# Taking the node tables' products apart in PSUM, with kv writes that wait for no window load

## The chip, the cores and the metric

The kernel runs on one core of one Trainium2 chip. The metric is the device time of one execution in microseconds (us). Three executions of the kernel before gave 5036.83, 5021.88 and 5028.19 us, so the median is 5028.19 us. One more execution was profiled: 5024.54 us, with a span of 5022.8 us from its first to its last instruction and a mean granted TensorE clock of 0.904.

## The reference

One layer of a graph network over 12,500 nodes with 128 features, 412,500 edges sorted by destination (each edge, its reverse and one loop per node), and 64 features per edge:

```
h, q, k, v = x @ Wn + bn, x @ Wq + bq, x @ Wk + bk, x @ Wv + bv
eh   = edge_features @ We + be
hmid = leaky_relu(concat(q[src], k[dst], eh) @ A1 + b1, 0.2)
s    = leaky_relu(hmid @ A2 + b2, 0.2).mean(-1)
w    = softmax(s over all edges)
out  = segment_sum(w * v[dst], by src)
y    = layernorm(x + gamma * norm(h + out) + beta)
```

Wq, Wk and We are multiplied with their parts of A1 once, on the chip, so that q, k and the edge part add up directly to the hidden layer. What the change touches is the node tables: for every node a row of k and v (256 numbers), a row of q (128) and a row of h (128). Rows of q, k and v are kept as three bf16 pieces whose sum is the float32 number: the first piece is the number rounded to bf16, the second the rest rounded, the third what is then left.

## The kernel before

**Stages.** Nodes lie in 98 blocks of 128; seven blocks (NB = 7) make one of 14 node groups (ng). Edges are cut into 403 groups of 1,024, in destination order, and the edge groups into six parts of 51 to 73 groups. While part p is spread out, part p-1 is reduced.

- Spreading out (`make`, called once per part): for each edge group, `load` fetches edge features, destinations and a window of 128 piece rows of the k, v table; `onehots`, `masked` and `places` on VectorE work out where each edge goes; `rows` on TensorE picks k, v with one-hot matrices and adds the edge part; `evacuate` copies the result to SBUF on ScalarE (tile `rec`, six buffers, four edge tiles each); and GpSimd issues one indirect DMA (L904, "scatter" below) for each of the eight edge tiles, into the table `rtab` of the part, ordered by source block.
- Reducing (`sums_of`, from part 1 on): for blocks of source nodes the rows of `rtab` are loaded again (`rt`, L1038), and TensorE, VectorE and ScalarE do the hidden layer, the scores, the softmax weights and the weighted sums. At the end `closing` does the two norms.

The load of the first `rt` of a part reads rows that all scatters of that part have written, so it waits for the last of them.

**The tables.** The k, v rows of node group 0 are made before everything else, by code that keeps the product in PSUM and takes it apart there (L686 to L695). The other 27 jobs, k, v of node groups 1 to 13 and then q, h of node groups 0 to 13, are the generator `tables()`, whose steps are strewn between the steps of part 0: a part's generator `make` yields six times per edge group, so part 0 has 306 steps, and the tables' 379 steps are spread evenly over the first 275 of them. The small tables on edges (`edges`, chunks of 52 edge groups) and the zero fills of `rtab` (L522) are strewn in the same way. All engines run their instructions in the order in which this interleaving emits them, and every DMA that is not a scatter is issued by the SP queue, in order.

A job of `tables()` before: load the seven blocks of x, transposed (L1519, two buffers). Per block one float32 matmul into PSUM (L1534, two buffers `ph`) and one VectorE add of the bias into the SBUF tile `ns` (L1539). Then `parts3` on the whole group: ScalarE rounds to bf16 (L1502), VectorE subtracts into `less` (L1507), ScalarE rounds, VectorE subtracts, ScalarE rounds. All pieces lie in the tile `sp`, which has one buffer. Then the writes: `kvtab` (L1547) for a k, v job, `htab` (L1557) and `qtab` (L1558) for a q, h job.

The window load of an edge group (L796) reads `kvtab` at a row that is known only at run time, so it counts as reading the whole table. A load therefore waits for the last `kvtab` write in front of it, and a `kvtab` write waits for all window loads in front of it. `made_rows` records how many node groups' rows were written when a load was issued; `covered` checks at the end that no window reached beyond.

## Time and profile before

| what | value |
|---|---|
| median of three runs | 5028.19 us |
| profiled execution | 5024.54 us, span 5022.8 us |
| busy: TensorE, VectorE, ScalarE, GpSimd | 4158.4, 3991.7, 3267.8, 3348.4 us |
| scatters (L904) | 3224, the first at 31.3 us, the last at 4331.6 us |
| scatters of part 0 | 408 of them (51 edge groups) |

Times in the rows are microseconds from the start of the span unless they are marked ns. A group's row gives the line, engine and operation, the tiles written and read, how often it ran, then busy time, mean duration in ns, and idle time of the engine in front of it with what ended that idle time. A row of stretches gives for each engine the busy time in the stretch and, in brackets, the instructions; then the granted TensorE clock, the share of time for which the 16 DMA engines were busy, and the GB/s moved. A row of waits gives who waited for what: microseconds in total, how often, the longest. "issue" marks time in which nothing that the profile shows was waited for.

### The profile page before, as it was taken

What the parts mean: (1) busy time and instruction counts of PE and PEld (TensorE: products, weight loads), DVE (VectorE), ACT (ScalarE), POOL (GpSimd) and SP (SyncE); (2) the same over time, 40 slices, a digit from 0 to 9 for tenths busy, and PEclk for the clock granted to TensorE, in tenths of its full rate; (3) what the DMA queues carried; (4) which work ended last, traced back from release to release, by engine and by line L of the source; (5) the groups of instructions that cost most, each with busy time, mean ns of one, the idle gap of its engine ahead of it and who ended that gap; (6) DMA issues with size and microseconds to landing.
All of it is one profiled execution on the core that took longest, in us unless ns stands there. A gap on an engine that the chain in (4) does not pass through costs nothing.

```text
span 5022.8 us, 97600 instructions
## 1 busy us (share of the span) xinstructions
PE 4158.4 (83%) x32218; PEld 3108.6 (62%) x32676; DVE 3991.7 (79%) x10036; ACT 3267.8 (65%) x8495; POOL 3348.4 (67%) x3268
## 2 busy tenths in 40 slices
PE   4565578898888888799998898999899999899980
PEld 3333356666566666577776676676667777667760
DVE  7877576788777777688888888888888888677778
ACT  3433255666566666577777777777677777677876
POOL 5777777777777777777777777777777777410002
PEclk7777588899999999899999999999999999999995
DMA  7999799998899988899989888989899999788763
GB/s 262 314 318 344 255 328 333 343 312 300 274 324 324 329 301 289 275 318 318 313 308 311 302 315 311 309 307 313 301 306 314 315 324 318 265 287 283 262 224 141
DMA packets 614992, 1505.49 MB, mean 300 GB/s; under 512 B 103587, under 2 KB 328246, under 8 KB 612681
## 3 DMA queue, kind: packets, MB, share of 16 engines
q1 hardware_dynamic: 459433, 1069.47, 65.0%
q0 software_dynamic: 154752, 429.39, 22.7%
q8 instruction: 259, 4.24, 0.3%
q14 instruction: 260, 2.13, 0.1%
q10 hardware_dynamic: 288, 0.26, 0.0%
HBM read 929.49 MB, written 608.37 MB: 306 GB/s over the span
## 4 chain that ended last, share of the span: by engine, by line
DMA 37%; PE 24%; DVE 16%; POOL 9%; issue 6%; ACT 6%; SPq 1%; DVEq 0%; ACTq 0%; POOLq 0%
DMA rtab<-rec,idx 14%; DMA rt<-rtab 13%; POOL rtab L904 9%; PE psm L1268 6%; DMA row<-slT 4%; PE ph L1116 4%; PE pkv L881 3%; PE ph L1107 3%; DMA rowB<-row 3%; DVE hm L1131 2%; PE psc L1144 2%; PE pkv L875 2%; ACT rec L892 2%; PE psm L1177 2%; ACT ohw L1239 2%
## 5 line engine op out<-in xcount | busy, mean ns | idle before, releaser
L904 POOL DMA_INDIRECT rtab<-rec,idx x3224 | 3286.2, 1019 | 1042.0 <-issue 781.0
L892 ACT ACTIVATE rec<-pkv 128x1024 f32<-128x1024 f32 x806 | 819.9, 1017 | 863.5 <-PE pkv L881 475.4
L1239 ACT ACTIVATE ohw<-ohs,w 128x128 f32<-128x128 bf16 x3822 | 1258.7, 400 | 58.4 <-DVE ohs L1225 47.9
L1268 PE MATMUL psm<-rt,ohw 128*128 128x128 f32 x7644 | 1158.6, 294 | 10.7 <-ACT ohw L1239 10.6
L1268 PEld LDWEIGHTS psm<-rt,ohw 128*128 128x128 f32 x7644 | 997.5, 200 | 59.5 <-ACT ohw L1239 17.7
L1127 ACT ACTIVATE hm<-ph 128x512 f32<-128x512 f32 (+1 forms) x1078 | 581.7, 540 | 461.6 <-PE ph L1116 429.0
L1116 PE MATMUL ph<-ohT,qs 128*128 128x512 bf16 (+3 forms) x3658 | 718.1, 312 | 25.5 <-issue 2.6
L1131 DVE TENSOR_TENSOR hm<-ph,hm 128x512 f32<-128x512 f32 (+1 forms) x1078 | 668.5, 620 | 83.3 <-ACT hm L1127 81.9
L875 PE MATMUL pkv<-kvs,ohd 128*128 128x256 bf16 x3224 | 531.4, 292 | 204.0 <-ACT rec L892 189.7
L1107 PE MATMUL ph<-ident,rt 128*128 128x128 f32 x3822 | 629.3, 283 | 45.8 <-DVE hm L1131 43.4
L881 PE MATMUL pkv<-WeS,eat 64*128 64x128 f32 x6448 | 633.6, 320 | 0.0
L1096 DVE TENSOR_SCALAR ohT<-rowB,iotaP 128x512 bf16<-128x512 uint8 (+1 forms) x1078 | 518.4, 481 | 102.1 <-DMA rowB<-row 97.2
L881 PEld LDWEIGHTS pkv<-WeS,eat 64*128 64x128 f32 x6448 | 467.9, 205 | 191.8 <-issue 184.9
L875 PEld LDWEIGHTS <-ohd 128*128 128x128 bf16 x3224 | 316.2, 103 | 317.5 <-issue 224.5
L1107 PEld LDWEIGHTS ph<-ident,rt 128*128 128x128 f32 x3822 | 471.9, 152 | 64.1 <-DVE hm L1131 51.0
L1116 PEld LDWEIGHTS <-qs 128*128 128x128 bf16 x4116 | 396.8, 100 | 129.4 <-issue 4.8
L1225 DVE TENSOR_TENSOR ohs<-iotaE,sl 128x512 bf16<-128x512 bf16 (+1 forms) x1078 | 427.1, 396 | 48.4 <-ACT ohw L1239 46.8
L844 DVE TENSOR_TENSOR ats<-pc,oh 128x792 f32<-128x792 f32 x403 | 392.1, 973 | 82.1 <-PE pc L826 76.9
L1144 PE MATMUL psc<-hm,A2s 128*32 128x512 f32 (+3 forms) x2352 | 337.7, 538 | 80.1 <-DVE slT L1075 75.9
L1177 PE MATMUL psm<-headsum,z 128*128 128x4 f32 (+1 forms) x2156 | 287.9, 255 | 128.0 <-DVE part L1284 87.0
L855 DVE TENSOR_REDUCE pos<-ats 128x8 f32<-128x792 f32 x403 | 390.2, 968 | 4.2
L1177 PEld LDWEIGHTS psm<-headsum,z 128*128 128x128 f32 (+1 forms) x2156 | 280.9, 202 | 149.4 <-DVE part L1284 102.6
(161 smaller groups left out, 4080.2 us busy)
## 6 DMA issues: line engine op xcount, KB each, us to landing
rt<-rtab SPq DMA_DIRECT2D x196, 1820.0 KB
eat<-in_ea SPq DMA_DIRECT2D x201, 512.0 KB
rt<-rtab SPq DMA_DIRECT2D x49, 1560.0 KB
rt<-rtab SPq DMA_DIRECT2D x49, 1300.0 KB
qs<-qtab SPq DMA_DIRECT2D x294, 192.0 KB
rtab<-rec,idx POOLq DMA_INDIRECT x3224
dstb<-dtab SPq DMA_DIRECT2D x201, 256.0 KB
rtab<-empty SPq DMA_DIRECT2D x98, 520.0 KB
```

Of the source, the lines that this page charges most:

```text
L875: nc.tensor.matmul(pk[:, h, i, :], ohd[:, t * P : (t + 1) * P], kvs, start=(i == 0), stop=False,)
L881: nc.tensor.matmul(pk[:, h, i, :D], eat[h * DE : (h + 1) * DE, (j + i) * P : (j + i + 1) * P], WeS[h * DE : (h + 1) * DE, :], start=False, ...
L892: nc.scalar.activation(rec[:, :, :, : 2 * D], pk, AF.Copy)
L904: one_tile = nc.gpsimd.indirect_dma_start(out=rtab[p % TABS][:, :], out_offset=bass.IndirectOffsetOnAxis(ap=idxs[g][:, t : t + 1], axis=0) ...
L1096: nc.vector.tensor_scalar(st["oh"][k][:, : n * P], st["rowB"][:, t0 * P : (t0 + n) * P], iotaP, None, op0=ALU.is_equal,)
L1107: nc.tensor.matmul(ph[:, j * P : (j + 1) * P], st["rt"][:, t0 + j, :D], ident, is_transpose=True, start=(j == 0), stop=False,)
L1116: nc.tensor.matmul(ph[:, cols], st["qs"][:, j0 // t, s, :], oh[:, cols], start=False, stop=(s == 2 and j1 == t0 + n),)
L1127: nc.scalar.activation(hm, state[i]["ph", k][:, : n * P], AF.Copy, scale=SLOPE)
L1131: nc.vector.tensor_tensor(hm, ph[:, : n * P], hm, op=ALU.max)
L1177: nc.tensor.matmul(st["psS"][:, t0 + j : t0 + j + (nv - 1) * sw + 1 : sw], z[: 32 * nv, j * P : (j + 1) * P], headsum[: 32 * nv, :nv], sta ...
L1239: nc.scalar.activation(ohw[:, j, :], ohs[:, :, j], AF.Copy, scale=st["w"][:, t0 + j : t0 + j + 1])
L1268: nc.tensor.matmul(st["psS"][:, (1 + u) * P : (2 + u) * P], ohw[:, j, :], st["rt"][:, t0 + j, D : 2 * D], start=(k == 0), stop=(k == t - 1),)
```

## The change

- **Products.** A job's seven blocks are now four products, of two, two, two and one blocks. A product's matmuls write one PSUM bank. Banks come in turn from the pools `ph` (twice), `psc` and `psm`, which have nothing else to do in part 0, so four products can be in flight.
- **Bias.** VectorE adds it in place in PSUM (`biased`): for k, v jobs to the v half alone (k's bias is zero in this formulation, as in the code for node group 0), for q, h jobs to both halves.
- **Pieces.** Per product: ScalarE rounds PSUM to `sp` (`rounded`), VectorE subtracts in place in PSUM (`left`, s = 0), ScalarE rounds again, VectorE subtracts from PSUM straight into the third piece of `sp` (`left`, s = 1). The tiles `ns` and `less` and the third rounding are gone. For q, h jobs ScalarE also copies h from PSUM to SBUF (`own`).
- **Order.** An explicit table of 225 slots, two per product, strewn like the 379 steps before over the first 275 steps of part 0: product at slot t, bias at t + 1, rounding at t + 2, first subtraction at t + 4, second rounding at t + 5, second subtraction at t + 6, and the job's writes two slots after its last subtraction. x is loaded eight slots, one job, ahead.
- **Buffers.** `sp` has two (`sp0`, `sp1`), h has two.
- **Waits on the k, v table.** A window load is told not to depend on writes of node groups from `ready[g]` on, and a `kvtab` write not to depend on any window load. `made_rows` now lags by one node group, so a load depends on writes up to the one before the latest. A no-op stands in front of each `kvtab` write on the SP queue.
- **Edge tables.** In `edges` the write of `dtab` (L609) is issued one step later, behind all four VectorE instructions instead of between them.

```diff
@@ -606,13 +606,13 @@
         )
         db = tmp.tile([size, EG], U8, name="db")
         nc.vector.tensor_scalar(db[:m, :], dI[:m, :], first[:m, :], None, op0=ALU.subtract)
-        nc.sync.dma_start(out=dtab[g0:g1, :], in_=db[:m, :])
         dl = tmp.tile([size, EG], BF, name="dl")
         nc.vector.tensor_scalar(dl[:m, :], dI[:m, :], first[:m, :], None, op0=ALU.subtract)
         row = tmp.tile([size, 1], I32, name="row")
         nc.vector.tensor_scalar(row[:m, :], first[:m, :], 3.0, None, op0=ALU.mult)
+        yield
+        nc.sync.dma_start(out=dtab[g0:g1, :], in_=db[:m, :])
         nc.sync.dma_start(out=stab[g0:g1, :], in_=row[:m, :])
-        yield
         nc.vector.tensor_reduce(mm[:m, 0, c : c + 1], dl[:m, :], AX.X, ALU.max)
         yield
         nc.vector.tensor_reduce(mm[:m, 1, c : c + 1], dl[:m, :], AX.X, ALU.min)
@@ -672,7 +672,7 @@
             psmp.tile([P, 4 * P], FP, name="psm"),
             pkvp.tile([P, 2, 2, 2 * D], FP, name="pkv").rearrange("p h i w -> p (h i w)"),
         ]
-        sp = np_.tile([P, NB, 3, 2, D], BF, name="sp")
+        sp = np_.tile([P, NB, 3, 2, D], BF, name="sp1")
         for b in range(0, NB, 2):
             m = min(2, NB - b)
             at = nodes[b // 2][:, : 2 * D * m]
@@ -793,10 +793,13 @@
                 skip_runtime_bounds_check_because="starts are held within the table on the chip",
             )
             kvs = kvp.tile([P, 2 * D], BF)
-            nc.sync.dma_start(
+            read = nc.sync.dma_start(
                 out=kvs,
                 in_=kvtab.rearrange("n (s w) -> (n s) w", s=3)[bass.ds(row, P), :],
-            )
+            ).ins
+            for c in range(max(ready[g], 1), ng):
+                tc.declare_no_dep(read, group=f"kv{c}", reason="a window in front of these rows")
+            tc.add_to_no_dep_group("kvs", read)
             data[g] = eat, dstb, kvs
 
         def onehots(g):
@@ -1496,68 +1499,108 @@
 
 
 
-    def parts3(to, rest, half):
-
-        for s in range(3):
-            nc.scalar.activation(to[s], rest, AF.Copy)
-            yield
-            if s < 2:
-                less = np_.tile([P, NB, 2, D], FP, name=f"less{s}")
-                less = less[:, :, :half, :]
-                nc.vector.tensor_tensor(less, rest, to[s], op=ALU.subtract)
-                rest = less
-                yield
-
     def tables():
+
         jobs = [(True, c) for c in range(1, ng)] + [(False, g) for g in range(ng)]
-        xts = {}
-
-        def load_x(i):
-            if i < len(jobs):
-                kv, g = jobs[i]
-                xts[i] = xp.tile([D, NB, P], FP, name="xt")
+        slots = {}
+
+        def do(at, fn, *args):
+            slots.setdefault(at, []).append((fn, args))
+
+        def load_x(job):
+            kv, g = job["of"]
+            job["xt"] = xp.tile([D, NB, P], FP, name="xt")
+            nc.sync.dma_start(
+                out=job["xt"], in_=xN[:, g, :, :] if kv else xT[:, g * NB : (g + 1) * NB, :]
+            )
+
+        def product(job, n, b, m):
+            kv, _ = job["of"]
+            if b == 0:
+                job["sp"] = np_.tile([P, NB, 3, 2, D], BF, name=f"sp{job['i'] % 2}")
+                if not kv:
+                    job["h"] = np_.tile([P, NB, D], FP, name=f"h{job['i'] % 2}")
+            from_pool, name = ((php, "ph"), (php, "ph"), (pscp, "psc"), (psmp, "psm"))[n % 4]
+            ph = from_pool.tile([P, 4 * P], FP, name=name)
+            w = Wkv if kv else Wqh
+            for k in range(m):
+                to = ph[:, 2 * D * k : 2 * D * (k + 1)]
+                nc.tensor.matmul(
+                    to, job["xt"][:, b + k, :], w.rearrange("k s d -> k (s d)"),
+                    start=(k == 0), stop=(k == m - 1),
+                )
+            job["ph", b] = ph[:, : 2 * D * m].rearrange("p (b t d) -> p b t d", b=m, t=2)
+
+        def biased(job, b, m):
+            kv, _ = job["of"]
+            at, bias = (
+                (job["ph", b][:, :, 1, :], bias_kv[:, 1:2, :].to_broadcast([P, m, D])) if kv
+                else (
+                    job["ph", b],
+                    bias_qh.rearrange("p (o s) d -> p o s d", o=1).to_broadcast([P, m, 2, D]),
+                )
+            )
+            nc.vector.tensor_tensor(at, at, bias, op=ALU.add)
+
+        def piece(job, b, m, s):
+            kv, _ = job["of"]
+            sp = job["sp"]
+            if kv:
+                return job["ph", b], sp[:, b : b + m, s, :, :]
+            sq = sp.rearrange("p b s t d -> p (b s t d)")[:, : NB * 3 * D].rearrange(
+                "p (b s o d) -> p b s o d", b=NB, s=3, o=1
+            )
+            return job["ph", b][:, :, 0:1, :], sq[:, b : b + m, s, :, :]
+
+        def rounded(job, b, m, s):
+            of, to = piece(job, b, m, s)
+            nc.scalar.activation(to, of, AF.Copy)
+
+        def own(job, b, m):
+            nc.scalar.activation(job["h"][:, b : b + m, :], job["ph", b][:, :, 1, :], AF.Copy)
+
+        def left(job, b, m, s):
+            of, less = piece(job, b, m, s)
+            to = of if s == 0 else piece(job, b, m, s + 1)[1]
+            nc.vector.tensor_tensor(to, of, less, op=ALU.subtract)
+
+        def put(job):
+            kv, g = job["of"]
+            sp = job["sp"].rearrange("p b s t d -> p (b s t d)")
+            if kv:
+                nc.sync.nop()
+                write = nc.sync.dma_start(out=kv_rows(g), in_=sp).ins
+                tc.declare_no_dep(write, group="kvs", reason="rows that no window has reached")
+                tc.add_to_no_dep_group(f"kv{g}", write)
+                made_rows[0] = g
+            else:
+                made_rows[0] = ng
+                bl = slice(g * NB, (g + 1) * NB)
+                nc.sync.dma_start(out=htab[:, bl, :], in_=job["h"])
                 nc.sync.dma_start(
-                    out=xts[i], in_=xN[:, g, :, :] if kv else xT[:, g * NB : (g + 1) * NB, :]
-                )
-
-        load_x(0)
-        yield
-        for i, (kv, g) in enumerate(jobs):
-            load_x(i + 1)
-            xt = xts.pop(i)
-            ns = np_.tile([P, NB, 2, D], FP, name=f"ns{i % 2}")
-            w, bias = (Wkv, bias_kv) if kv else (Wqh, bias_qh)
-            for j in range(NB + 1):
-                before = ph if j else None
-                if j < NB:
-                    ph = php.tile([P, 4 * P], FP, name="ph")
-                    nc.tensor.matmul(
-                        ph[:, : 2 * D], xt[:, j, :], w.rearrange("k s d -> k (s d)"),
-                        start=True, stop=True,
-                    )
-                if j:
-                    nc.vector.tensor_tensor(
-                        ns[:, j - 1, :, :].rearrange("p s d -> p (s d)"), before[:, : 2 * D],
-                        bias.rearrange("p s d -> p (s d)"), op=ALU.add,
-                    )
-                yield
-            sp = np_.tile([P, NB, 3, 2, D], BF, name="sp")
-            if kv:
-                yield from parts3([sp[:, :, s, :, :] for s in range(3)], ns, 2)
-                nc.sync.dma_start(
-                    out=kv_rows(g), in_=sp.rearrange("p b s t d -> p (b s t d)")
-                )
-                made_rows[0] = g + 1
-            else:
-                sq = sp.rearrange("p b s t d -> p (b s t d)")[:, : NB * 3 * D].rearrange(
-                    "p (b s o d) -> p b s o d", b=NB, s=3, o=1
-                )
-                yield from parts3([sq[:, :, s, :, :] for s in range(3)], ns[:, :, 0:1, :], 1)
-                bl = slice(g * NB, (g + 1) * NB)
-                nc.sync.dma_start(out=htab[:, bl, :], in_=ns[:, :, 1, :])
-                nc.sync.dma_start(
-                    out=qtab[:, bl, :], in_=sq.rearrange("p b s o d -> p b (s o d)")
-                )
+                    out=qtab[:, bl, :],
+                    in_=sp[:, : NB * 3 * D].rearrange("p (b w) -> p b w", b=NB),
+                )
+
+        n = 0
+        for i, of in enumerate(jobs):
+            job = dict(of=of, i=i)
+            do(max(2 * n - 8, 0), load_x, job)
+            for b in range(0, NB, 2):
+                m, t = min(2, NB - b), 2 * n
+                do(t, product, job, n, b, m)
+                do(t + 1, biased, job, b, m)
+                do(t + 2, rounded, job, b, m, 0)
+                if not of[0]:
+                    do(t + 2, own, job, b, m)
+                do(t + 4, left, job, b, m, 0)
+                do(t + 5, rounded, job, b, m, 1)
+                do(t + 6, left, job, b, m, 1)
+                n += 1
+            do(t + 8, put, job)
+        for t in range(max(slots) + 1):
+            for fn, args in slots.get(t, []):
+                fn(*args)
             yield
 
     def later():
@@ -1606,7 +1649,7 @@
                     for j, piece in enumerate(pieces)
                 ]
             fills = fills[::-1]
-            tabs, made, nt = tables() if p == 0 else iter(()), 0, 1 + (2 * ng - 1) * (NB + 7)
+            tabs, made, nt = tables() if p == 0 else iter(()), 0, 2 * (2 * ng - 1) * -(-NB // 2) + 9
             more, sent, ne = later() if p == 0 else iter(()), 0, 11 * (len(chunks) - 1)
             for i, _ in enumerate(a):
                 if p == 0 and i == 60:
```

## The prediction

> **What bounds the kernel now.** I read the page's engine shares and slices first, then the scatters by stretch, then their single rows, then who waits for whom in part 0, because the change touches nothing behind part 0.
>
> ```profile
> PE 4158.4 (83%) x32218; PEld 3108.6 (62%) x32676; DVE 3991.7 (79%) x10036; ACT 3267.8 (65%) x8495; POOL 3348.4 (67%) x3268
> ...
> POOL 5777777777777777777777777777777777410002
> ...
> L904 POOL DMA_INDIRECT rtab<-rec,idx x3224 | 3286.2, 1019 | 1042.0 <-issue 781.0
> ```
>
> GpSimd has only 67% of the span as busy time, but its slices stand at 7 without a dip from the second to the 34th and never more. The group row says why: 781.0 of its 1042.0 us of idle time are "issue", a fixed gap that no other engine causes. The single rows further down show the gap as 0.30 us in front of a scatter of 0.96 us, so 1.26 us per scatter is the fastest pace that the trace shows. The scatters by stretch (first column the stretch, then its length, GpSimd's busy time and count) compare part 0 with what follows:
>
> ```profile
> 60.00:300.00 240.00, 187.23 (x160) 0.73 0.97 313
> 300.00:565.00 265.00, 202.05 (x193) 0.72 1.02 342
> 1600.00:4000.00 2400.00, 1843.38 (x1826) 0.95 0.90 308
> ```
>
> Between 60 and 565 us, while tables are made, 353 scatters take 505 us, 1.43 us each; between 1600 and 4000 us it is 2400/1826 = 1.31. At 1.26 us they would take 445 us, so 60 us of these 505 lie above the floor. Nearly all of it is GpSimd running long rather than waiting. Mean durations are 187.23/160 = 1.170 us (k, v jobs), 202.05/193 = 1.047 us (mostly q, h jobs) and 1843.38/1826 = 1.010 us later. Over the 0.96 us of an undisturbed scatter that is 33.6 + 16.8 = 50 us; the other 10 us are real waits, and the table of GpSimd's waits in 60 to 565 us holds them:
>
> ```profile
> POOL rtab L904 <- DMA rtab<-rec,idx: 8.8, 21, 1.8
> POOL rtab L904 <- ACT rec L893: 6.0, 9, 3.0
> ```
>
> (These totals include the 0.30 us gap of each.) So GpSimd bounds part 0, with almost no slack. What makes scatters long is in the timeline:
>
> ```profile
> 264.38 2.02 DVE L1507 TENSOR_TENSOR less<-ns,sp 128x1792 f32<-128x1792 f32 x1 [1.55 <-ACT sp L1502]
> 264.47 2.76 POOL L904 DMA_INDIRECT rtab<-rec,idx  x1 [0.30 <-issue]
> ...
> 268.18 2.01 DVE L1507 TENSOR_TENSOR less<-less,sp 128x1792 f32<-128x1792 f32 x1
> 268.80 2.35 POOL L904 DMA_INDIRECT rtab<-rec,idx  x1 [0.30 <-issue]
> ...
> 281.55 0.96 DVE L844 TENSOR_TENSOR ats<-pc,oh 128x792 f32<-128x792 f32 x1
> 281.68 0.96 POOL L904 DMA_INDIRECT rtab<-rec,idx  x1 [0.30 <-issue]
> ```
>
> The first subtraction (L1507, both inputs in SBUF) ends at 266.40, and the scatter that began with it ends at 267.23. The second ends at 270.19, its scatter at 271.15, exactly 0.96 us later: the scatter does its work only when the subtraction is over. The last pair is the contrast: L844 reads PSUM and SBUF, and the scatter beside it takes its 0.96 us.
>
> Does a shorter part 0 shorten the whole? Its end is fixed by scatters:
>
> ```profile
> 617.22 0.96 POOL L904 DMA_INDIRECT rtab<-rec,idx  x1 [0.30 <-DMA rtab<-rec,idx]
> ...
> 620.96 0.38 SPq L1038 DMA_DIRECT2D rt<-rtab  x1
> ```
>
> The 408th scatter starts at 617.22; the first load of part 1's reduction (L1038), which had to wait for it, goes out at 620.96 and the rest of the kernel, unchanged by the edit, is ordered behind it. So I carry every microsecond won in part 0 to the end.
>
> **The change part by part.** First VectorE's subtractions. These rows, from the groups by shape over 0 to 565 us, hold the old work and, by L686 to L695, the new form, which node group 0 already uses:
>
> ```profile
> L1539 DVE TENSOR_TENSOR ns<-ph,hm 128x256 f32<-128x256 f32 x189 | 76.2, 417 | 47.1 <-PE ph L1534 46.6
> L1507 DVE TENSOR_TENSOR less<-ns,sp 128x1792 f32<-128x1792 f32 x13 | 26.3, 2023 | 8.7 <-ACT sp L1502 8.7
> L1507 DVE TENSOR_TENSOR less<-less,sp 128x1792 f32<-128x1792 f32 x13 | 26.3, 2021 | 9.6 <-ACT sp L1502 9.6
> L1507 DVE TENSOR_TENSOR less<-ns,sp 128x896 f32<-128x896 f32 x14 | 15.3, 1091 | 32.4 <-ACT sp L1502 32.4
> L1507 DVE TENSOR_TENSOR less<-less,sp 128x896 f32<-128x896 f32 x14 | 15.1, 1078 | 2.0 <-ACT sp L1502 2.0
> ...
> L695 DVE TENSOR_TENSOR ph<-ph,sp 128x512 f32<-128x512 f32 x2 | 1.3, 676 | 0.0
> L695 DVE TENSOR_TENSOR sp<-ph,sp 128x512 bf16<-128x512 f32 x2 | 1.3, 669 | 0.0
> L686 DVE TENSOR_TENSOR ph<-ph,bias 128x256 f32<-128x256 f32 x2 | 0.7, 412 | 0.0
> L695 DVE TENSOR_TENSOR pkv<-pkv,sp 128x256 f32<-128x256 f32 x1 | 0.4, 410 | 0.0
> L686 DVE TENSOR_TENSOR pkv<-pkv,bias 128x128 f32<-128x128 f32 x1 | 0.3, 277 | 0.0
> ```
>
> A k, v job before: 7 x 0.417 + 2.023 + 2.021 = 6.96 us. After: biases 3 x 0.412 + 0.277, subtractions 3 x 0.676 + 0.410 and 3 x 0.669 + 0.41, together 6.37 us. A q, h job before: 7 x 0.417 + 1.091 + 1.078 = 5.09 us. After: biases over both halves 3 x 0.676 + 0.410 = 2.44 us, two subtractions of 3 x 0.410 + 0.277 each, 5.45 us. Over 13 and 14 jobs: 13 x (-0.59) + 14 x 0.36 = -2.6 us of VectorE time, nothing. The gain is in the place of the operands: all 54 L1507 instructions, 83 us, go, and no new VectorE instruction has two SBUF inputs. How much of the 50 us goes? Bounds: nothing, if the scatters are long for another reason (a loss is excluded for this term, since nothing is added that holds GpSimd in these rows); 50 us if all go back to 0.96. I take the 1600 to 4000 us row as the nearest, since scatters run there beside VectorE work without table subtractions: from 1.170 and 1.047 down to 1.010 gives 160 x 0.160 + 193 x 0.037 = 33 us.
>
> On this the Trainium skill says two things ("SBUF — State Buffer", The single rule and Practical consequences). A VectorE instruction with two SBUF inputs blocks a GpSimd instruction that reads SBUF, for its whole length; the rows above agree (ends 0.83 and 0.96 us after). But the same section infers that a tensor_tensor does not hold up descriptor writing, since it takes only the read side; by that alone the term would be zero. The rows here decide for the first.
>
> Second, the supply must keep up, or GpSimd waits instead. ScalarE makes the records (L892) between the table work, in order. Its waits for VectorE and for writes in 60 to 565 us, and VectorE's for it:
>
> ```profile
> ACT sp L1502 <- DVE less L1507: 85.5, 45, 9.6
> ACT sp L1502 <- DMA qtab<-sp: 51.8, 10, 9.8
> ACT sp L1502 <- DMA kvtab<-sp: 8.7, 2, 6.6
> ...
> DVE less L1507 <- ACT sp L1502: 52.2, 29, 6.2
> ```
>
> With `sp` in two buffers the waits for landing writes go, 51.8 + 8.7 = 60.5 us on ScalarE, ahead of records on the same queue. To follow GpSimd the supply must gain 33 us of 505, so 60 us is cover enough. Late next are the handoffs between VectorE and ScalarE, now per product. ScalarE's busy time grows: a k, v job from 3 x 1.697 to 2 x (3 x 0.596 + 0.394) = 4.36 us, a q, h job from 3 x 0.950 to at most 3 x 4 x 0.394 = 4.73 us, in all 13 x (-0.73) + 14 x 1.88 = +17 us.
>
> ```profile
> L1502 ACT ACTIVATE sp<-ns 128x1792 bf16<-128x1792 f32 x13 | 22.1, 1696 | 20.0 <-issue 11.8 <-DVE ns L1539 4.2 <-DMA kvtab<-sp 2.1
> L1502 ACT ACTIVATE sp<-ns 128x896 bf16<-128x896 f32 x14 | 13.3, 950 | 62.1 <-DMA qtab<-sp 51.8 <-DMA kvtab<-sp 6.6 <-issue 1.5
> L693 ACT ACTIVATE sp<-ph 128x512 bf16<-128x512 f32 x4 | 2.3, 596 | 11.5 <-DVE ph L686 10.7 <-DVE ph L695 0.7
> L693 ACT ACTIVATE sp<-pkv 128x256 bf16<-128x256 f32 x2 | 0.8, 394 | 1.5 <-DVE pkv L695 1.5
> ...
> 60.00:300.00 240.00, 145.63 (x778) 95.59 (x775) 197.51 (x363) 105.74 (x120) 187.23 (x160) 0.73 0.97 313
> 300.00:565.00 265.00, 151.14 (x830) 99.55 (x829) 192.42 (x390) 90.52 (x136) 202.05 (x193) 0.72 1.02 342
> ...
> 360.00:380.00 20.00, 12.30 (x70) 8.17 (x70) 14.00 (x31) 6.17 (x10) 15.43 (x16) 0.67 1.05 377
> ```
>
> ScalarE is busy 105.74 + 90.52 = 196 of 505 us; 213 fit. VectorE is busy 197.51 + 192.42 = 390 us; in 505 - 33 = 472 us that is 82%, which leaves 82 us for waits. TensorE's matmuls stay the same, 297 us of busy time; they gain banks, since four products fly where two matmuls did.
>
> Third, the SP queue:
>
> ```profile
> SPq L1547 <- DMA kvs<-kvtab: 62.9, 13, 9.4
> SPq L609 <- DVE db L608: 18.3, 4, 8.1
> SPq L796 <- DMA kvtab<-sp: 17.8, 7, 4.2
> ```
>
> The independent k, v writes and the later `dtab` write take away 62.9 + 17.8 + 18.3 = 99 us of standing still. I give it nothing: in the waits of the other engines no load of edge features or windows appears, so these stalls were covered by loading four edge groups ahead. The no-op in front of 13 writes is below anything here; x one job ahead can only help. The lag of `made_rows` makes loads wait for older writes alone. Bounds: nothing, or, if a standing queue did hold up an engine unseen, those 99 us, which the 10 us of real waits on GpSimd cut to 10. I take nothing, since no wait row names such a load.
>
> Sum: 33 us from GpSimd's pace, 0 from the rest. The profiled execution's 5024.5 becomes 4991.5; the median shown lies 3.7 us above that execution, so I say 4995 us.
>
> **The rivals.** *GpSimd is not released, or the supply does not follow.* If the supply keeps its pace, the scatters get shorter and GpSimd idles as much more. The 10 us of waits say that the supply is only just sufficient today. Then the gain is 0 to 10 us: about 5023 us.
>
> *The DMA engines become the bound.* Their share is 0.97 and 1.02 in the two stretches, moving 313 and 342 GB/s. Against it: the stretch 360 to 380 us carries 377 GB/s at 1.05 with 16 scatters in 20 us, the floor pace. If 1.05 is the ceiling, 505 us can shrink to 240 x 0.97/1.05 + 265 x 1.02/1.05 = 479: 26 us won, 5002 us.
>
> *Slower: handoffs on the in-order VectorE queue.* Each of 108 products now has two VectorE instructions that stand behind a rounding on ScalarE, 216 against 54 before. Today such a wait averages 52.2/29 = 1.8 us where it occurs, 1.0 us over 54. At 1.0 us each, 216 us would stand against the 505 - 390 = 115 us that VectorE has free: +101 us, 5129 us. It decides from 115/216 = 0.53 us on. Against it: one to two slots, 505/225 = 2.2 us each, lie between a rounding and its subtraction.
>
> **How the numbers follow.** A measurement here tells a change of about 0.3%, 15 us, from none. Forecast 4995 us: chance 0.62, own range 4975 to 5012. DMA bound, 5002 us: 0.12. No release or no supply, 5023 us: 0.17, no change. Handoffs, 5129 us: 0.09, slower. So faster 0.74, same 0.17, slower 0.09. The range goes from 4968 us (all 60 us above the floor won) to 5028 us and leaves out the slower case and little more.
>
> **What would show it.** Right: mean scatter duration in part 0 near 1.01 us, no long scatters beside table subtractions; the 408th scatter and the first `rt` load some 33 us earlier; ScalarE with no wait for a `qtab` write; the same distance from that load to the end. Wrong: GpSimd's waits for records growing by tens of us (supply), waits for its own earlier scatters growing (DMA), VectorE's waits for ScalarE above 115 us (handoffs), or long scatters beside instructions with PSUM operands. A later part that ran slower by what part 0 won would break the carrying-over.

## The result and the profile after

The changed kernel takes 5000.0 us in the median of 5 runs (4996.21 to 5003.54), the kernel before 5025.78 us in 5 runs beside it (5021.88 to 5036.83). The ratio is 0.9941 with a 95% interval of 0.9930 to 0.9951. It is faster, by 25 to 35 us (0.49% to 0.70% of 5025.78); 4995 us had been forecast. The profiled execution took 4997.18 us (span 4995.4) against 5024.54 (span 5022.8).

From the page of the changed kernel, the engines' shares, GpSimd's slices and the scatters (now L907):

```profile
PE 4185.0 (84%) x32676; PEld 3106.9 (62%) x32676; DVE 3984.1 (80%) x10117; ACT 3260.1 (65%) x8686; POOL 3315.9 (66%) x3268
...
POOL 5777777777777777777777777777777777310002
...
L907 POOL DMA_INDIRECT rtab<-rec,idx x3224 | 3253.2, 1009 | 1046.2 <-issue 778.6
```

The page hardly shows the change: GpSimd is busy 32.5 us less, its idle time is nearly the same, and its last stretch of work ends a fraction of a slice earlier. The stretches show where it happened (changed kernel; stretch, its length, then busy time and count of PE, PEld, DVE, ACT and POOL, then clock, DMA share, GB/s):

```profile
60.00:300.00 240.00, 162.47 (x872) 107.22 (x871) 210.66 (x459) 106.30 (x223) 177.48 (x179) 0.75 1.02 353
300.00:565.00 265.00, 153.20 (x870) 103.35 (x870) 187.75 (x430) 93.81 (x236) 198.69 (x199) 0.68 0.93 323
1600.00:4000.00 2400.00, 2179.77 (x17764) 1638.29 (x17761) 1992.17 (x4882) 1692.08 (x4487) 1843.61 (x1824) 0.95 0.90 308
```

The same 505 us of part 0 now hold 179 + 199 = 378 scatters instead of 353, and the stretch behind it is as it was (1824 against 1826). One scatter and its gap took 505/353 = 1.431 us and take 505/378 = 1.336. I split this into the mean duration and the mean gap in front of it, since the two say different things: a long duration is a scatter that is held, a long gap (0.30 us is the floor) is one that waits. (The kernel issues a no-op in front of every scatter, and no run shows what share of the 0.30 us is its.) Duration: 389.28/353 = 1.103 before (the sum of the two rows shown of before), 376.17/378 = 0.995 after. Gap: (505 - 389.28)/353 = 0.328 before, (505 - 376.17)/378 = 0.341 after. Over 353 scatters that is 38 us won in duration and 5 us lost in gaps, 33 us together.

The scatters beside the new subtractions, from the timeline of the changed kernel (start, duration):

```profile
107.53 0.68 DVE L1565 TENSOR_TENSOR ph<-ph,sp 128x512 f32<-128x512 f32 x1
...
107.69 0.96 POOL L907 DMA_INDIRECT rtab<-rec,idx  x1 [0.30 <-issue]
...
111.03 0.69 DVE L1565 TENSOR_TENSOR ph<-ph,sp 128x512 f32<-128x512 f32 x1
111.49 0.96 POOL L907 DMA_INDIRECT rtab<-rec,idx  x1 [0.30 <-issue]
...
584.10 0.96 POOL L907 DMA_INDIRECT rtab<-rec,idx  x1 [0.30 <-issue]
...
586.57 0.38 SPq L1041 DMA_DIRECT2D rt<-rtab  x1
```

Both scatters begin inside a subtraction and take their 0.96 us. Between 60 and 565 us 78 scatters begin inside one of the new subtractions, and only one of them is 0.04 us or more above 0.96. Part 0 ends 620.96 - 586.57 = 34.4 us earlier.

The waits in 60 to 565 us (total, times, longest), changed kernel:

```profile
ACT sp L1557 <- DMA qtab<-sp: 71.9, 11, 11.0
...
DVE sp L1565 <- ACT sp L1557: 44.2, 17, 9.3
PE pc L829 <- DVE few L821: 43.9, 31, 6.4
...
ACT sp L1557 <- DMA kvtab<-sp: 42.0, 9, 8.1
ACT rec L895 <- PE pkv L884: 36.1, 26, 3.0
...
ACT rec L895 <- DMA rtab<-rec,idx: 25.6, 11, 6.4
...
POOL rtab L907 <- DMA rtab<-rec,idx: 12.8, 34, 1.4
...
POOL rtab L907 <- ACT sp L1557: 10.0, 17, 5.2
...
SPq L619 <- DMA stab<-row: 40.4, 6, 11.1
```

And three rows of the kernel before, from the same view, that the prediction left out:

```profile
ACT rec L892 <- PE pkv L881: 141.0, 42, 7.8
...
PE pc L826 <- DVE few L818: 66.4, 19, 10.7
...
PE ph L1534 <- DVE ns L1539: 39.7, 28, 6.4
```

ScalarE's waits for landing table writes did not go: 60.5 us before, 71.9 + 42.0 = 113.9 us after, in spite of the second buffer. What went is its wait for TensorE in front of a record, from 141.0 to 36.1 us. And it now waits 25.6 us for scatters to give record buffers back, against 1.4 us before: part of the time the records are ahead of GpSimd.

### The profile page after: what moved, and what is told of

Same layout as the page of the kernel before. It is cut to its first block, busy times and chain, and to the rows that moved or that the text cites. A ratio compares the mean times of both kernels' runs of the same rounds, so it can differ in the third digit from the quotient of the medians.

```text
span 4995.4 us, 98371 instructions
## 1 busy us (share of the span) xinstructions
PE 4185.0 (84%) x32676; PEld 3106.9 (62%) x32676; DVE 3984.1 (80%) x10117; ACT 3260.1 (65%) x8686; POOL 3315.9 (66%) x3268
## 4 chain that ended last, share of the span: by engine, by line
DMA 35%; PE 23%; DVE 15%; POOL 12%; issue 7%; ACT 6%; SPq 1%; ACTq 0%; DVEq 0%; POOLq 0%
DMA rtab<-rec,idx 17%; POOL rtab L907 12%; DMA rt<-rtab 8%; PE psm L1271 6%; DMA row<-slT 4%; PE ph L1119 4%; DMA rowB<-row 3%; PE pkv L884 3%; PE ph L1110 3%; ACT rec L895 2%; PE psc L1147 2%; DVE hm L1134 2%; PE pkv L878 2%; ACT ohw L1242 2%; PE psm L1180 2%
## 5 line engine op out<-in xcount | busy, mean ns | idle before, releaser
L907 POOL DMA_INDIRECT rtab<-rec,idx x3224 | 3253.2, 1009 | 1046.2 <-issue 778.6
L895 ACT ACTIVATE rec<-pkv 128x1024 f32<-128x1024 f32 x806 | 821.9, 1020 | 876.0 <-DMA rtab<-rec,idx 550.4
L1119 PE MATMUL ph<-ohT,qs 128*128 128x256 bf16 (+3 forms) x4116 | 819.7, 321 | 0.0
L1228 DVE TENSOR_TENSOR ohs<-iotaE,sl 128x512 bf16<-128x512 bf16 (+1 forms) x1078 | 430.0, 399 | 68.3 <-ACT ohw L1242 66.4
```

The source lines that it names most:

```text
L895: nc.scalar.activation(rec[:, :, :, : 2 * D], pk, AF.Copy)
L907: one_tile = nc.gpsimd.indirect_dma_start(out=rtab[p % TABS][:, :], out_offset=bass.IndirectOffsetOnAxis(ap=idxs[g][:, t : t + 1], axis=0) ...
L1119: nc.tensor.matmul(ph[:, cols], st["qs"][:, j0 // t, s, :], oh[:, cols], start=False, stop=(s == 2 and j1 == t0 + n),)
```

## The experiments

All ratios are to the kernel before, on the same chip in the same batch. Its medians there were 5033.23 us (runs 1 to 4), 5027.99 us (5 to 8) and 5031.19 us (9 to 12), so runs of different batches, the changed kernel among them, are compared by their ratios and not by their times. The first load of `rt` marks the end of part 0; like the columns before it, it comes from one profiled execution of each kernel. Scatters, durations and gaps are worked out as above, from each profile's two rows for 60 to 300 and 300 to 565 us.

| kernel | scatters in 505 us | duration, us | gap, us | first `rt` load | ratio (95%) |
|---|---|---|---|---|---|
| before | 353 | 1.103 | 0.328 | 620.96 | 1 |
| after | 378 | 0.995 | 0.341 | 586.57 | 0.9941 (0.9930 to 0.9951) |
| 1 after, operands in SBUF | 376 | 1.022 | 0.321 | 591.70 | 0.9953 (0.9937 to 0.9969) |
| 2 before, two `sp` | 356 | 1.100 | 0.318 | 620.15 | 0.9998 (0.9988 to 1.0007) |
| 3 after, k, v waits back | 370 | 0.991 | 0.374 | 598.33 | 0.9955 (0.9939 to 0.9971) |
| 4 after, `dtab` early | 373 | 0.986 | 0.367 | 595.21 | 0.9957 (0.9945 to 0.9969) |
| 5 before, split subtractions | 359 | 1.020 | 0.387 | 616.51 | 1.0001 (0.9991 to 1.0011) |
| 6 after, long dose | 364 | 1.064 | 0.323 | 607.96 | 0.9978 (0.9968 to 0.9988) |
| 7 after, short dose | 376 | 1.015 | 0.328 | 591.03 | 0.9956 (0.9941 to 0.9970) |
| 8 after, PSUM dose | 376 | 0.994 | 0.349 | 589.81 | 0.9940 (0.9924 to 0.9957) |
| 9 before, split, two `sp`, SP queue | 359 | 1.028 | 0.379 | 615.28 | 0.9985 (0.9973 to 0.9996) |
| 10 as 9, four banks | 364 | 1.027 | 0.361 | 606.17 | 0.9965 (0.9950 to 0.9979) |
| 11 after, three `sp` | 379 | 0.985 | 0.347 | 587.19 | 0.9936 (0.9923 to 0.9950) |
| 12 as 11, edge loads spread | 381 | 0.992 | 0.333 | 583.47 | 0.9929 (0.9917 to 0.9941) |

**1. The place of the operands.** The changed kernel, but the bias goes from PSUM into an SBUF tile per job, and both subtractions read that tile and `sp`, still per product. Two things come with it: the addition covers both halves in k, v jobs too, and ScalarE's copy of h is not needed.

```diff
-            nc.vector.tensor_tensor(at, at, bias, op=ALU.add)
+            nc.vector.tensor_tensor(
+                job["ns"][:, b : b + m, :, :], job["ph", b],
+                (bias_kv if kv else bias_qh).rearrange("p (o s) d -> p o s d", o=1)
+                .to_broadcast([P, m, 2, D]), op=ALU.add,
+            )
+            job["ph", b] = job["ns"][:, b : b + m, :, :]
```

> The changed kernel, but the bias is added from PSUM into an SBUF tile and both subtractions then have two SBUF inputs; products, banks, order, two buffers and waits stay. Theory P (the gain is scatters that VectorE's two-SBUF-input subtractions no longer hold up): a hold of 0.69 us meets a scatter start in 0.69/1.26 of the cases and costs 0.35 us then, so 6 x 0.19 + 2 x 0.07 = 1.3 us per k, v job and 0.4 us per q, h job, some 22 us in all: about 5022 us, scatters in part 0 above 1.04 us on average. Theory W (the gain is the products in flight, the second buffers and the free SP queue): as the changed kernel, about 5000 us, scatters at 1.00 us.

The first `rt` load comes 5.1 us later than in the changed kernel, and the time, 5005.11 us (0.9953), cannot be told from its; it is nearer the 5000 us of theory W than the 5022 us of theory P. The mean duration rises by 0.027 us only, 0.027 x 376 = 10 us of hold. So two SBUF inputs alone, in short pieces, bring back about a quarter of the 38 us in duration, and half of that reaches the end of part 0.

**2. Two buffers alone.** The kernel before with `name=f"sp{i % 2}"`.

> The kernel before with one edit: two buffers for sp, so that ScalarE's first rounding of a job no longer waits for the write of the job before. Theory P: GpSimd stays held by the same subtractions, so 5018 to 5026 us, scatters in 60 to 300 us still near 1.17 us. Theory W: the 60 us of ScalarE's waits for qtab and kvtab writes were what held the supply back, so 20 us or more are won: 5005 us or less.

5030.78 us, ratio 0.9998: nothing. ScalarE's 60.5 us of waits for landing writes of `sp` are gone in this run, so they were not what held up part 0.

**3 and 4. The SP queue, undone in the changed kernel.** In 3 the k, v writes wait again for the window loads in front of them (`declare_no_dep` and its groups go, `made_rows[0] = g + 1`). In 4 the `dtab` write is issued behind the instruction that makes `db`, as before, and the `stab` write, which the change had issued one step later along with it, is in its old place too:

```diff
         nc.vector.tensor_scalar(db[:m, :], dI[:m, :], first[:m, :], None, op0=ALU.subtract)
+        nc.sync.dma_start(out=dtab[g0:g1, :], in_=db[:m, :])
...
+        nc.sync.dma_start(out=stab[g0:g1, :], in_=row[:m, :])
         yield
-        nc.sync.dma_start(out=dtab[g0:g1, :], in_=db[:m, :])
-        nc.sync.dma_start(out=stab[g0:g1, :], in_=row[:m, :])
```

> The changed kernel with the waits between k, v writes and window loads as before. Theory P: the stalls of the SP queue were covered, so within 5 us of the changed kernel, 4997 to 5005 us, although the SP queue stands still some 60 us more. Theory W: the queue's stalls delay loads and cost 10 to 30 us: 5010 to 5030 us.

> The changed kernel with the dtab write issued where it was before, between the VectorE instructions. Theory P: nothing, 4997 to 5005 us. Theory W: the SP queue waits some 18 us more for VectorE and up to 10 us of it come through: up to 5010 us.

5007.92 and 5008.23 us. The waits on SP's queue in 60 to 565 us, first run 3, then run 4:

```profile
SPq L1569 <- DMA kvs<-kvtab: 69.9, 13, 8.5
...
SPq L796 <- DMA kvtab<-sp: 37.4, 8, 6.7
```

```profile
SPq L609 <- DVE db L608: 42.5, 6, 10.9
```

The stalls are back (run 3's also include waits for rows just written). Over all rows of this view except that of the first `rt` load, SP stands 278 and 294 us, against 264 in the changed kernel. The wait behind the `stab` write, 40.4 us in the changed kernel, is 6.1 us in run 4, where that write comes a step earlier. The first `rt` load is 11.8 and 8.6 us later than in the changed kernel, and it is the gap that has grown (0.374 and 0.367 against 0.341), not the duration. That records come late because SP stands is the likely reading, and no run traces a single late record back to it. In the time, 0.9955 and 0.9957 against 0.9941 would be 7 to 8 us each, but the intervals overlap, so a cost in the time is not shown.

**5. Release without the rest.** The kernel before; only the subtraction over a node group is issued in four pieces, of two, two, two and one of its blocks:

```diff
-                nc.vector.tensor_tensor(less, rest, to[s], op=ALU.subtract)
+                for b in range(0, NB, 2):
+                    nc.vector.tensor_tensor(
+                        less[:, b : min(b + 2, NB)], rest[:, b : min(b + 2, NB)], to[s][:, b : min(b + 2, NB)], op=ALU.subtract
+                    )
```

> The kernel before with each table subtraction (both inputs in SBUF) issued in four pieces of 2, 2, 2 and 1 node groups, one right behind the other; nothing else is changed, the sum is the same. Theory length (a scatter is held for what is left of the one VectorE instruction it meets, and slips in between two pieces): mean scatter duration in 60 to 300 us falls from 1.170 to about 1.05 us, as where the subtractions of the changed kernel had their inputs in SBUF (1.051); the first rt load comes up to 15 us earlier, if the records follow. Theory operands (what counts is the sum of VectorE time with two SBUF inputs): mean stays at 1.15 us or more and the time within 5 us of the kernel before. Theory supply (records and not scatters set the pace of part 0 before): the mean falls, but GpSimd waits as much longer and the time stays within 5 us.

5027.49 us, ratio 1.0001. Two rows of the stretches and two of GpSimd's waits:

```profile
60.00:300.00 240.00, 141.98 (x767) 92.76 (x767) 201.74 (x433) 105.78 (x120) 173.54 (x167) 0.74 0.95 318
300.00:565.00 265.00, 160.96 (x865) 105.40 (x865) 203.18 (x484) 91.25 (x138) 192.49 (x192) 0.72 1.01 343
```

```profile
POOL rtab L904 <- ACT rec L893: 27.7, 20, 5.6
...
POOL rtab L904 <- DVE ohd L820: 7.1, 2, 4.6
```

The scatters are released (173.54/167 = 1.039 us in the first stretch, 1.170 before), with the same operands in the same place. But GpSimd now waits 27.7 us for records where it waited 6.0; part 0 ends 4.5 us earlier, and no gain shows in the time. Both the theory of length and the theory of supply are borne out: the kernel before had two limits at nearly the same pace.

**6, 7 and 8. Doses.** The changed kernel with a useless addition: one of 128x1792 per job (6), or one as wide as the product for each product, on two SBUF inputs (7) or on the product in PSUM and an SBUF tile (8). The output is untouched. The three variants side by side, shortened:

```diff
+        def dose(job, b, m):
+            dz = slots["dz"]
+            nc.vector.tensor_tensor(dz, dz, dz, op=ALU.add)                      # 6, if b == 0
+            nc.vector.tensor_tensor(dz[:, :w], dz[:, :w], dz[:, :w], op=ALU.add)  # 7, w = 2 * D * m
+            nc.vector.tensor_tensor(dz[:, :w], product, dz[:, :w], op=ALU.add)    # 8
...
                 do(t + 5, rounded, job, b, m, 1)
+                do(t + 3, dose, job, b, m)
```

> The changed kernel with one useless VectorE addition of 128x1792 fp32, both inputs in SBUF, per table job (27 in all, some 2.0 us each, 54 us of VectorE time) at the slot before the first subtraction of the job. Theory hold: each of the 27 delays the scatter beside it by about 1.1 us, mean scatter duration in part 0 back to 1.05 to 1.10 us; first rt load 20 to 31 us later than in the changed kernel. Theory load (only VectorE's time counts): the same as the dose with PSUM input, per us of VectorE time.

> The changed kernel with one useless VectorE addition of 128x512 (last product of a job: 128x256) fp32, both inputs in SBUF, per product: 108 pieces, in all about the same VectorE time as the long dose. Theory hold by length: a short piece costs a scatter 0.1 us or less, 27 x (3 x 0.1 + 0.04) = 9 us in all; mean scatter duration about 1.02 us. Theory operands: as many us of hold as in the long dose, 20 to 31 us.

> Control for the two doses: the same 108 additions, but one input of each is the product in PSUM. VectorE's load is that of the short dose or a little over it (some 67 us of 505), the hold is none. Theory hold: mean scatter duration as in the changed kernel, 0.99 us; the first rt load moves only by what VectorE's load costs. If this run is as slow as the doses with SBUF inputs, they show load and not hold.

5016.63, 5002.15 and 4997.28 us. A line's summary in run 6 and in run 7 (duration least/median/most in ns, first and last start):

```profile
L1572 DVE TENSOR_TENSOR dz<-dz x27: 1954/2015/2031, 45.3 to 497.9; 128x1792 f32<-128x1792 f32 x27
```

```profile
L1572 DVE TENSOR_TENSOR dz<-dz x108: 406/678/727, 43.8 to 513.9; 128x512 f32<-128x512 f32 x81, 128x256 f32<-128x256 f32 x27
```

27 x 2.015 = 54 us of long instructions, about 81 x 0.678 + 27 x 0.41 = 66 us of short ones. In the timeline, run 6 first:

```profile
129.80 2.02 DVE L1572 TENSOR_TENSOR dz<-dz 128x1792 f32<-128x1792 f32 x1
...
130.51 2.14 POOL L907 DMA_INDIRECT rtab<-rec,idx  x1 [0.31 <-issue]
```

```profile
61.31 0.96 POOL L907 DMA_INDIRECT rtab<-rec,idx  x1 [0.30 <-issue]
...
61.63 0.67 DVE L1572 TENSOR_TENSOR dz<-dz 128x512 f32<-128x512 f32 x1
...
62.58 0.96 POOL L907 DMA_INDIRECT rtab<-rec,idx  x1 [0.30 <-issue]
...
87.42 0.69 DVE L1572 TENSOR_TENSOR dz<-dz 128x512 f32<-128x512 f32 x1
...
87.64 1.30 POOL L907 DMA_INDIRECT rtab<-rec,idx  x1 [0.30 <-issue]
```

The rule of the single row is the same in both: the long instruction ends at 131.82 and its scatter at 132.65, the short one at 88.11 and its scatter at 88.94, 0.83 us later each. But the short one at 61.63 lies between two starts of scatters, 1.27 us apart, and holds neither. A scatter that starts inside the instruction is held for what is left of it. Of the long ones 26 of 27 contain a start, and leave much; of the 81 pieces of 128x512 only 35 do, and leave little. Added up over the scatters between 60 and 565 us that start inside a dose, the time above 0.96 us is 26.7 us in run 6 (25 scatters, all held), 7.7 us in run 7 (38, 28 of them held) and nothing in run 8 (43, none held). Over all scatters of the stretch, whatever they lie beside, it is 39.5, 22.2 and 13.6 us, against 13.2 in the changed kernel: 26.3, 9.0 and 0.4 us more. The end of part 0 moves by 21.4, 4.5 and 3.2 us, and the ratio of run 6 lies clear of the changed kernel's while those of 7 and 8 do not. Run 8 is the control: 56 us more of VectorE work in 505 us (its busy time rises from 398 to 454 us) cost nothing that shows in the time, so the loss in run 6 is the hold and not the load.

**9 and 10. What feeds the scatters.** Run 9 is the kernel before with everything of the change that lies outside the pipeline of the products: split subtractions, two `sp`, independent k, v writes, the later `dtab` and `stab` writes, `made_rows` behind. Run 10 adds four banks in turn for the products:

```diff
-                    ph = php.tile([P, 4 * P], FP, name="ph")
+                    of, name = ((php, "ph"), (php, "ph"), (pscp, "psc"), (psmp, "psm"))[(i * NB + j) % 4]
+                    ph = of.tile([P, 4 * P], FP, name=name)
```

> The kernel before with its tables as they were (groups of seven products, sums in SBUF), the subtractions in four pieces, two sp buffers, and everything that the change does on the SP queue: k, v writes with no wait for loads in front, the dtab write one step later, made_rows one group behind. Only the pipeline of the products in PSUM is left out. Theory SP queue (the records were late in the kernel before because SP stood still in front of the loads): GpSimd's waits for records vanish and the first rt load comes 15 to 25 us earlier than in the kernel before, time 5000 to 5010 us. Theory pipeline (records were late because TensorE and VectorE, in order, stood at the products and groups of the tables): GpSimd still waits 25 us or more for records, time within 7 us of the kernel before.

> The run before this one with the products of the tables in four banks in turn instead of two, still one bank per product and one instruction for bias on each. Theory banks (TensorE's 40 us of waits for the bias of the product two back hold up the records): these waits go and the first rt load comes another 10 us earlier. Theory handoffs (it is the chain of rounding and subtracting over a whole group that stands in the order of VectorE and ScalarE): within 4 us of the run before this one.

5026.85 and 5018.89 us. Waits of GpSimd, TensorE and SP's queue in run 9, then of the first two in run 10:

```profile
POOL rtab L907 <- ACT rec L896: 26.1, 16, 7.5
...
PE pc L829 <- DVE few L821: 67.8, 19, 13.7
...
PE ph L1540 <- DVE ns L1545: 43.3, 30, 6.8
...
SPq L1554 <- ACT sp L1505: 76.4, 10, 12.2
```

```profile
POOL rtab L907 <- ACT rec L896: 15.2, 10, 6.9
...
PE pc L829 <- DVE few L821: 79.4, 26, 15.0
```

In run 9 GpSimd waits for records as in run 5, and the time is where the theory of the pipeline had it. The k, v write no longer stands behind loaded windows, but it stands 76.4 us behind ScalarE's parts instead: what was late next on SP's queue was the pipeline of the tables itself. In run 10 TensorE's 43.3 us at the bias of the product two back are gone, GpSimd's wait falls by 11 us and part 0 ends 9.1 us earlier, as the theory of banks had it (the intervals of the two ratios overlap). From there to the changed kernel are 606.17 - 586.57 = 19.6 us more. They belong to what is left of the change: bias and subtractions in PSUM per product, two products to a bank, spread over slots. The table splits them: the duration falls from 1.027 to 0.995, over 364 scatters 12 us, and the gap from 0.361 to 0.341, 7 us. So the larger part is once more scatters that are no longer held, about what run 1 gives for the place of the operands (10 us), and the smaller part is supply. TensorE's wait for the one-hots of the edge work (L829), which stand on VectorE's queue among the table work, goes from 79.4 to 43.9 us there. ScalarE's idle time in front of the records' main copy (L892 before, L895 in the other two) is 142 us before, 131 in run 10 and 71 in the changed kernel; what it waited for is less sure, since the trace puts 141.0 us of it down to TensorE before and 117.2 us to "issue" in run 10. No run separates the parts of the supply further.

**11 and 12. Is there more to have?** Run 11 has three `sp` buffers. Run 12 has in addition one step more between the load of the edge numbers and its first reader, and two between the write to `stab` and the load from it, one of them taken from behind the load.

> The changed kernel with three sp buffers. ScalarE's waits for landing writes (71.9 + 42.0 = 114 us in 60 to 565 us) should go. Theory slack (GpSimd bounds part 0, records lie ready 10 to 20 us): the first rt load within 3 us of the changed kernel's 586.57, time the same. Theory supply (the records are still late at times): GpSimd's 10 us of waits for ScalarE's sp go and the time falls by 5 to 10 us.

> The run before this one, and the chunks of edge numbers take two steps more: one between their load and the first instruction that reads it (VectorE waits 24.0 us for dI in the changed kernel), and one between the write of row to stab and the load of start from it (SP stands 40.4 us behind that write). Theory slack: time as in the changed kernel, 4997 to 5000 us. Theory supply: GpSimd's last waits for records go, first rt load 5 to 10 us earlier, time some 4992 us.

5001.64 us (0.9936) and 4999.60 us (0.9929, 0.9917 to 0.9941). Run 11: part 0 ends where it did, and the waits for landing writes have moved from `sp` to the buffers of `h`:

```profile
ACT h L1560 <- DMA htab<-h: 57.0, 11, 10.5
```

Run 12, waits of ScalarE and GpSimd:

```profile
ACT rec L897 <- DMA rtab<-rec,idx: 132.7, 43, 7.1
...
POOL rtab L909 <- DMA rtab<-rec,idx: 18.3, 38, 2.1
...
POOL rtab L909 <- ACT sp L1559: 3.7, 12, 0.3
```

ScalarE waits 132.7 us for record buffers, GpSimd hardly at all for records: the supply is now plentiful, and part 0 ends 3.1 us earlier than in the changed kernel. The interval of the time overlaps the changed kernel's, so a gain over it is not shown. GpSimd bounds part 0 at 505/381 = 1.325 us per scatter, against the floor of 1.26.

## Why the prediction was right

The forecast was 4995 us, the measured median is 5000.0, and the mechanism named for the likeliest case, scatters that VectorE's subtractions no longer hold, is the one that decides. Steps behind it were wrong all the same, and that they add up to nearly the right sum is in part luck.

- **GpSimd bounds part 0, and L1507 holds it: right.** Of the 50.5 us above 0.96 us in the kernel before, 37.2 are those of scatters that start inside an L1507 subtraction; in the changed kernel 13.2 us are left, 0.2 of them from scatters that start inside L1565. The term was 33 us, since I stopped at the later stretch's 1.010; the duration fell to 0.995, worth 38 us, of which 5 us went into longer gaps. That this comes to 33 again is luck. The end at 0.96 us after the subtraction, from one pair of rows, was an exception: over all scatters that start inside L1507 the median is 0.83 us.
- **"The gain is in the place of the operands": only half the reason.** Run 1 keeps two SBUF inputs and ends part 0 only 5.1 us later, run 5 keeps them and releases most scatters, and run 7 adds 66 us of them for 7.7 us of holding. What held the scatters was that the instructions with two SBUF inputs were long. The change removed both properties at once. Shortness alone takes the mean duration from 1.103 to 1.020 (run 5), most of the way to 0.995; the rest, some 10 us, goes with the place of the operands (run 1). A long instruction with a PSUM operand was not run; the longest that the traces have beside a scatter, L844 with 0.96 us, leaves it alone.
- **"With `sp` in two buffers the waits for landing writes go", 60.5 us: wrong.** In the old pipeline they do go (run 2). In the changed kernel they grew to 113.9 us. The write of job i is issued in slot 8i + 14, and job i + 2 rounds into the same buffer in slot 8i + 18: four slots of 505/225 = 2.2 us, 9 us in which the write has to land. Run 2 shows that they were not the limit anyway, and run 11 that removing them from `sp` moves nothing. So "60 us is cover enough" named the wrong wait.
- **The supply came from a row that the argument had left out.** The longest wait of ScalarE was in front of a record, 141.0 us, put down to TensorE, with TensorE in turn at the products' banks (39.7 us) and at VectorE's one-hots (66.4 us). The prediction wrote of the banks only that "they gain banks". Runs 9 and 10 put 9 us of part 0 on the banks; of the 19.6 us that come with the rest of the pipeline some 7 are supply.
- **SP's queue, 99 us of stalls taken away and put at nothing: not so simple.** The three waits go, but others come: over all rows without the first `rt` load SP stands 235 us before and 264 after, 40.4 of it behind the `stab` write (6.9 before), which the change issues one step later along with the `dtab` write. Undone one at a time, the two parts of the change cost 11.8 and 8.6 us at the end of part 0 of one execution each; in the time no cost is shown. In the old pipeline they are worth 1.2 us there (run 9 against run 5, with the second `sp`; the times, 0.9985 and 1.0001, have intervals that overlap). So they seem to have a price only where the rest of the supply is fast: the cover that I named, loads four groups ahead, fits the kernel before, and for the one after it is doubtful.
- **Part 0's end is carried through: right within what one execution shows.** The first `rt` load came 34.4 us earlier (about 33 forecast), the span is 27.4 us shorter. From that load to the end of the span are 4401.8 us before and 4408.8 after; in the twelve runs, which do not differ behind part 0, it is between 4402.3 and 4417.8. So the 7 us lie within what single executions differ by. One number was misread: 617.22 is the start of the 407th scatter, the 408th starts at 618.48.
- **The rivals.** "Not released, or the supply does not follow" is what run 5 does, 1.0001: for the release alone it would have been the right forecast. The DMA bound gave 5002 us, near the result, but its sign is missing: GpSimd's waits for its own earlier scatters are 12.8 us over 34 times, of which 34 x 0.30 = 10.2 are the fixed gap. Handoffs: VectorE waits 44.2 us for ScalarE, less than the 52.2 before and far from the 115 that decide. In the other direction ScalarE's roundings wait 116 us for VectorE's table work, against 91 before.
- **The two statements of the Trainium skill** ("SBUF — State Buffer", Who interferes with whom) need not contradict each other here. It lets a VectorE instruction with two SBUF inputs contend with a GpSimd instruction that reads SBUF; the rows agree, since all 26 scatters that start inside a long addition of run 6 end 0.83 to 0.84 us after it. Its inference that a tensor_tensor leaves descriptor writing alone is not tested: by its rows a scatter reads the tile `idx` besides `rec`, and no run parts that reading from the writing of descriptors.

## What to carry to other kernels

Split what GpSimd does in a stretch into mean duration and mean gap: the first shows what holds it, the second what feeds it, and a change that mends only one of two limits at the same pace may show no gain (run 5, ratio 1.0001). Before a supply is called sufficient, take the longest wait of the engine that makes it, whatever the change is about, and follow it one engine further. Beside GpSimd's scatters, cut long VectorE instructions with two SBUF inputs into short ones; moving an operand into PSUM besides took away some 10 us of hold here, 5 us of them at the end of part 0 (run 1).

## What the runs showed of the hardware

The hold goes by the length of the single VectorE instruction, not by the sum: 54 us in pieces of 2.0 us held scatters for 26.7 us, 66 us in pieces of 0.68 and 0.41 us for 7.7 us, and about the same with one PSUM input not at all (43 scatters started inside one). I had not expected pieces issued right behind one another to do as well as pieces spread out (first stretch: 1.039 us in run 5, 182.95/174 = 1.051 us in run 1).

A second buffer behind DMA writes is no cover by itself: with the DMA engines at a share of 0.93 to 1.02, ScalarE still waited up to 11.0 us at a time until the write of the job before last had left the buffer.
